# Keys of the pick stage read from PSUM instead of SBUF, with two product buffers instead of three

## The chip, the cores and the metric

The kernel runs on one core of one Trainium2 chip. The metric is device time in microseconds (us) of one execution, and smaller is better. The kernel before takes 2175.24 us, the median of 9 runs (2168.76 to 2190.18).

The engines are named as in the profile: PE (TensorE; PEld is its weight load), DVE (VectorE), ACT (ScalarE), POOL (GpSimd) and SP (SyncE, which here only issues DMAs).

## The reference

One graph layer over N = 6250 nodes and E = 200000 edges, sorted by their destination:

```python
w = silu(edge_attr @ W1 + b1) @ W2 + b2                 # (E, 9), edge_attr (E, 32)
h_src = features[src]                                    # (E, 64), rows of x
msg = einsum('ef,em,fmg->eg', h_src, edge_sh * w, W_tp)  # (E, 64)
agg = segment_sum(msg, dst, N) / sqrt(AVG_DEG)
emb = silu(c_noise[:, None] @ Wn1 + bn1) @ Wn2 + bn2     # gamma, beta per node
x = layernorm(x + agg * (1 + gamma) + beta)
```

The part that matters here is `features[src]`: for each edge a row of 64 floats is fetched by index.

## The kernel before, in words

The edges are cut into tiles of 128 and the tiles into 98 groups (`NBLK`) of 16 (`KB`). A group's source rows stand in one SBUF tile `hs` of 128 x 16 x 64 floats. They come there in three ways:

- by gather: `gather(g)` (line 101) issues one indirect DMA per tile on POOL, 1152 in all. Its tile `hs` has `AHEAD + 1` = 7 buffers, so the gathers of group i + 6 wait until PE has read group i - 1 (`windows`, line 611);
- by 128 single-row DMAs on SP for one tile of every fourth group (`load_rows`, line 117);
- by picking, for the last 4 tiles of a group (3 in group 0 and in the groups of `FEW`; 388 in all). All of x lies in SBUF, split into two parts `xs`. A source index is a pair: a key, which says in which of 7 x 128 rows a block of 7 nodes lies, and a number `jl` from 0 to 6 in the block.

A pick has three steps. `hots` (line 558, DVE) compares the 128 keys of a tile with `nk` for all 7 x 128 rows, which gives a 0/1 matrix `hot_k` of 128 x 896 (7 buffers). `pick` (line 573, PE) multiplies it with `xs` in 14 matmuls of 448 columns that add up in a PSUM tile `px`; `px` has 3 buffers, each one bank. Then DVE masks `px` with `jl` into `xm` (line 582) and sums `xm` over 7 into `hs` (line 584). When `xm` is written, the buffer of `px` is free.

The keys come from DRAM: `load_keys` (line 488) reads them as float16 for two groups at a time, the same on all partitions, into `kr` (2 buffers). Only groups 0 and 1 take theirs from PSUM (`keys_first`), where matmuls have written them as float32.

The remaining work of a group: `hidden` (line 505, PE, then Silu on ACT, lines 510 and 516), `second` (line 525), `weights` on DVE (its last step `a`, line 544), `windows` (line 611), which multiplies rows and weights into `pzw`, copies of `pzw` on ACT (line 625), `project` and `place` (lines 661, 665 and 675) for each pair of groups, and the ending of node blocks (lines 864 to 881).

The order of the work is written by hand (`tc.manual_schedule`); the engines work through it in that order, each on its own. One turn i of the main loop is, on PE: `pick(i+1, 0)`; `middle(i)`, which is `project` or its transpose, `hidden(i+2)`, `second(i+1)` and `windows(i)`; then `pick(i+1, 1)`, `pick(i+1, 2)` and `pick(i+1, 3)`. On DVE it is `hots(i+2)` for tiles 0 and 1, the mask and sum of pick 0, `hots(i+2)` for tiles 2 and 3, `weights(i+1)`, then the masks and sums of picks 1 to 3. On POOL it is the 11 to 13 gathers of group i + 6.

[...]

Of the kernel before, what the change touches and what calls it, by code (L numbers as in the profile page):

```python
# [7 lines left out]
F32 = mybir.dt.float32  # L8
# [8 lines left out]
P = 128  # L17
N, F, M, D, H, E = 6250, 64, 9, 32, 64, 200000
# [4 lines left out]
NBLK = (NT + KB - 1) // KB  # L23
W = 7
KW = KB * W
ZT = 8
# [3 lines left out]
Q = 4  # L30
J = 7
# [1 line left out]
SPG = range(7, NBLK, SPS)  # L33
SPR = P // SPS
EPS = 1e-5
FEW = range(NBLK - 7, NBLK - 2, 2)

KH = 8
NROW = NPAD + P
# [13 lines left out]
def picked(g):  # L53

    return Q - (g == 0 or g in FEW)

# [12 lines left out]
def gnn_resnorm_kernel(ctx: ExitStack, tc: tile.TileContext, x, src, dst, dst_row, ea, sh, cn,  # L69
                       w1, b1, w2, b2, wtp, wn1, bn1, wn2, bn2, out):  # L70
    nc = tc.nc
# [16 lines left out]
    with ExitStack() as fast:  # L88
# [4 lines left out]
        psum = fast.enter_context(tc.tile_pool(name="psum", bufs=1, space=bass.MemoryType.PSUM))  # L93
# [101 lines left out]
        def setup(temp):  # L195
# [68 lines left out]
            def keys_first(g, kf, pk, act=False):  # L264

                pk_t[g] = pk
                spread = []
                for t in range(picked(g)):
                    c = (g + 1) * Q - picked(g) + t
                    d0 = NBLK * KB + c * P  # L270
                    dg = xb.rearrange("p j f -> p (j f)")[:, d0:d0 + P]
                    if act:
                        nc.scalar.mul(dg, ident, kf[:, c:c + 1])
                    else:
                        nc.vector.tensor_scalar(dg, ident, kf[:, c:c + 1], None, op0=ALU.mult)
                    spread.append(lambda t=t, dg=dg: nc.tensor.matmul(pk_t[g][:, t, :], ones, dg,
                                                                      start=True, stop=True))
                return spread
# [9 lines left out]
            kb = [ztw[:, k * LB * Q:(k + 1) * LB * Q] for k in range(6)]  # L288
# [3 lines left out]
                f()  # L292
            high(0)
            low(0)
            spread = keys_first(1, kb[0], psum.tile([P, Q, P], F32, tag="px", name="pk1", bufs=3), act=True)
            hots(0, 0, 1)
            for h in range(1, J):
                high(h)
# [62 lines left out]
            windows(0)  # L361
            second(1)
            hots(1, 3, Q)
            for k in range(2):
                nc.scalar.copy(ht[k][H:H + 1], ones[H:H + 1, None, :].to_broadcast([1, 4, P]))
            pick(1, 2)
# [183 lines left out]

        pk_t = {}

        def hots(g, t0, t1):

            for t in range(t0, min(t1, picked(g))):
                hot_k[g, t] = late.tile([P, J, P], F32R, tag="hot_k", name=f"hot_k{g}_{t}", bufs=7)
                keys = pk_t[g] if g in pk_t else kr_t[g]
                nc.vector.tensor_tensor(hot_k[g, t], keys[:, t, None, :].to_broadcast([P, J, P]),  # L558
                                        nk.unsqueeze(2).to_broadcast([P, J, P]), op=ALU.is_equal)

        def pick(g, t, other=()):


            other = [f for fs in other for f in fs]
            q = picked(g) if g < NBLK else 0
            if t >= q:
                for f in other:
                    f()
                return
            px = psum.tile([P, F, J], F32, tag="px", name=f"px{g}_{t}", bufs=3)  # L570
            for h in range(J):
                for i in range(2):
                    nc.tensor.matmul(px.rearrange("p f l -> p (f l)"), hot_k[g, t][:, h, :],  # L573
                                     xs[i][:, h].rearrange("p f l -> p (f l)"),
                                     start=(h == 0 and i == 0), stop=(h == J - 1 and i == 1))
                    if i == 1 and other:
                        other.pop(0)()
            for f in other:
                f()
            xm = late.tile([P, F, J], F32, tag="xm", name=f"xm{g}_{t}")  # L580
            c = (g + 1) * Q - q + t
            nc.vector.scalar_tensor_tensor(xm, li[:, None, :].to_broadcast([P, F, J]), jl[:, c:c + 1], px,  # L582
                                           op0=ALU.is_equal, op1=ALU.mult)
            nc.vector.tensor_reduce(hs[g][:, tiles(g) - q + t, :], xm, AX.X, ALU.add)  # L584
# [7 lines left out]
        def windows(g, k0s=None, last=None):  # L592

            nk = tiles(g)
            end = g == NBLK - 1
            hsg, ag = hs[g], a[g]
            z = zs[g] if g in zs else sums(g)


            for k0 in range(0, nk, ZT) if k0s is None else k0s:  # L600
                n = min(ZT, nk - k0)
                k1 = 0
                if last is not None:
                    n, k1 = (n, n - 1) if last else (n - 1, 0)
                pz = [pzw[k0 // ZT][:, 0:ZT // 2 * M * W].rearrange("p (k m w) -> p k m w", m=M, w=W)] * 2
                if end and last is not False:
                    pe = psum.tile([P, ZT // 2, M, W], F32, tag="px", name=f"pz{g}_{k0 + k1}_", bufs=3)
                    pz = [pe if last else pz[0], pe]
                for k in range(k1, n):
                    v = k % 2  # L610
                    mm = nc.tensor.matmul(pz[v][v * F:(v + 1) * F, k // 2].rearrange("p m w -> p (m w)"),  # L611
                                          hsg[:, k0 + k, :], ag[:, k0 + k].rearrange("p m w -> p (m w)"),
                                          start=True, stop=True)
                    if k0 + k == 0:

                        for d in hs_dma.pop(g)[(g not in SPG):]:
                            tc.add_manual_dep(mm.ins, d.ins.name, mybir.DependencyInfo(
                                mybir.DependencyClass.Sync, mybir.DependencyReason.DATA), reason="rows of the group")
                for v in range(2):
                    for h in range(2):  # L620
                        k = k1 + (v - k1) % 2
                        if k >= n:
                            continue
                        copy = nc.vector.tensor_copy if last is False else nc.scalar.copy
                        copy(  # L625
                            z[h * F:(h + 1) * F, 0:5 - h, k0 + k:k0 + n:2, :].rearrange("p m k w -> p k m w"),
                            pz[v][v * F:(v + 1) * F, k // 2:(n + 1 - v) // 2, h:M:2, :])
# [120 lines left out]
        with tc.manual_schedule(), tc.tile_pool(name="temp", bufs=1) as temp:  # L748
# [6 lines left out]
            for i in range(1, NBLK):  # L755
                if i + AHEAD < NBLK:
                    gather(i + AHEAD)
                if i % LB == 0 and i + LB < NBLK:
                    near(i + LB)
                if i % LB == 1 and i + 1 + LB < NBLK:  # L760
                    load(i + 1 + LB)
                    load_keys(i + 1 + LB)
                if i % 4 == 3 and i + 1 < NJ:
                    gate_load(i + 1)
                for g in SPG:
                    if AHEAD - SPS < g - i <= AHEAD:
                        load_rows(g, (AHEAD - g + i) * SPR)
                while tables:
                    tables.pop()()
                while stores:  # L770
                    stores.pop(0)()
                more = []
                if i + 2 < NBLK:
                    more = [lambda: hots(i + 2, 0, 2)]
                pick(i + 1, 0, [nodes(i), more])
                if i + 2 < NBLK:
                    hots(i + 2, 2, Q)
                if 56 <= i <= 58:
                    reach(i - 56)
                if i == NBLK - 2:  # L780
                    break
                reads = middle(i)
                if i % 4 == 1 and i - 1 < NJ:
                    gate_hidden(i - 1)
                pick(i + 1, 1, [weights(i + 1)])
                for f in reads:
                    f()
                beside = more_of.pop(i, [])
                n = -(-len(beside) // (Q - 1))
                for t in range(2, Q + 1):  # L790
                    for f in beside[(t - 2) * n:(t - 1) * n]:
                        f()
                    if t < Q:
                        pick(i + 1, t)
                    if t == 2 and i == NBLK - 3:
                        late_turn(i + 1, NBLK // 2 - 4)
                    if t in (2, 3) and ends:
                        ends.pop(0)()
                if i in (3, 5):
                    tables.append(keys_turn(LB + KC * (i - 1) // 2, kb[0], kt))  # L800
# [4 lines left out]
            nc.scalar.activation(root, eps, AF.Sqrt)  # L805
            windows(g - 1)
            pick(g, 1, [weights(g)])
            py = psum.tile([P, 1, F], F32, tag="s", name="py_l")
            for f in bring(q - 2, q - 1, py):
                f()  # L810
            finish(q - 2, q - 1, py)
# [249 lines left out]
```

## Time and profile before

| what | value |
|---|---|
| median of 9 runs | 2175.24 us (2168.76 to 2190.18) |
| the profiled execution | 2161.79 us, its span 2160.0 us |
| busy: PE / DVE / ACT / POOL | 1756.0 / 1233.8 / 515.4 / 1142.5 us |
| gathers (line 101) | 1152, mean 991 ns |
| picks' matmuls (line 573) | 5432, 1186.3 us busy |
| `hot_k` from `kr` (line 558) | 381, mean 1084 ns |
| mean granted clock of TensorE | 0.864 |

Each row of a group of instructions gives line, engine, operation and tiles (out<-in), count, then busy time and mean duration, then the time for which the engine sat idle just before them and what ended that. In the timeline a row gives the start and the duration in us, then engine, line and operation. "remote" is a wait whose releaser the profile doesn't know; "issue" is time in which the engine waited for nothing that the profile shows. Ends of matmuls are modelled.

### The profile page before, as it was taken

How to read it: one execution, taken by the hardware profiler on the slowest of the kernel's cores; microseconds unless marked ns; L12 is line 12 of the kernel's file. 1: busy time of each engine (PE TensorE's matmuls, PEld its weight loads, DVE VectorE, ACT ScalarE, POOL GpSimd, SP SyncE). 2: the span in 40 equal slices, each digit the busy share in tenths (PEclk: the TensorE clock that was granted, in tenths of full speed). 3: DMA queues.
4: the chain of work that ended last, by engine and by line, in shares of the span. 5: the costliest groups of instructions: out<-in, count | busy, mean ns of one | idle time of the engine just before them, and what ended most of it. 6: DMA issues, size and time to landing. Idle time of an engine off the chain costs nothing.

```text
span 2160.0 us, 37200 instructions
## 1 busy us (share of the span) xinstructions
PE 1756.0 (81%) x12273; PEld 1412.1 (65%) x12273; DVE 1233.8 (57%) x2228; ACT 515.4 (24%) x1427; POOL 1142.5 (53%) x1161
## 2 busy tenths in 40 slices
PE   4067888888888878888888888888888887888898
PEld 3056766666676767676767666666666666666677
DVE  3055565656565646556565556565646564646587
ACT  2022121312222212223122212121222121212233
POOL 7745546455555556455555554545555555555510
PEclk7568989899988989898989898988888988888899
DMA  4121211111121112111111111111111111111110
GB/s 127 35 61 40 59 36 42 45 49 40 39 56 41 38 39 59 35 41 39 57 37 39 48 45 36 39 38 54 37 39 50 42 37 38 54 38 36 39 44 5
DMA packets 89776, 95.75 MB, mean 44 GB/s; under 512 B 36504, under 2 KB 51050, under 8 KB 89578
## 3 DMA queue, kind: packets, MB, share of 16 engines
q1 hardware_dynamic: 52138, 53.89, 8.0%
q0 software_dynamic: 36864, 37.82, 7.8%
q8 instruction: 99, 1.62, 0.3%
q10 hardware_dynamic: 576, 1.61, 0.2%
q14 instruction: 99, 0.81, 0.1%
HBM read 91.49 MB, written 1.73 MB: 43 GB/s over the span
## 4 chain that ended last, share of the span: by engine, by line
PE 72%; issue 17%; another core or an unknown queue 4%; DVE 4%; POOL 2%; DMA 0%; ACT 0%; DVEq 0%; ACTq 0%; POOLq 0%
PE px L573 48%; PE pzw L611 7%; PE p L525 5%; PE p L661 4%; PE p L505 4%; PE pzw L505 2%; POOL hs L101 2%; DVE xm L582 1%; DVE hot_k L558 1%; DVE hs L584 1%; PE p L713 0%; PE ps L675 0%; DVE a L544 0%; PE p L690 0%
## 5 line engine op out<-in xcount | busy, mean ns | idle before, releaser
L101 POOL DMA_INDIRECT hs<-in_x_dram,src_i x1152 | 1141.2, 991 | 926.4 <-PE pzw L611 595.3
L573 PE MATMUL px<-xs_w,hot_k 128*128 128x448 f32 x5432 | 1186.3, 376 | 31.2 <-issue 29.0
L573 PEld LDWEIGHTS px<-xs_w,hot_k 128*128 128x128 f32 x5432 | 1042.2, 195 | 124.2 <-issue 35.0
L582 DVE SCALAR_TENSOR_TENSOR xm<-li,jl,px 128x448 f32<-128x448 f32 x388 | 262.9, 678 | 849.0 <-remote 591.3
L558 DVE TENSOR_TENSOR hot_k<-kr,nk 128x896 fp32r<-128x896 f16 x381 | 397.5, 1084 | 0.0
L510 ACT ACTIVATE st<-p,b1c 128x512 f32<-128x512 f32 x98 | 67.4, 688 | 798.1 <-remote 439.4
L584 DVE TENSOR_REDUCE hs<-xm 128x64 f32<-128x448 f32 x388 | 240.6, 620 | 13.4
L625 ACT COPY ztw<-pzw 64x140 f32<-64x140 f32 (+1 forms) x778 | 209.3, 269 | 45.3 <-PE pzw L611 32.9
L661 PE MATMUL p<-ztw,wtc 128*64 128x112 f32 x940 | 107.8, 328 | 128.5 <-issue 128.2
L505 PE MATMUL pzw<-ea,w1bd 32*64 32x256 f32 x784 | 130.9, 541 | 96.5 <-issue 95.7
L611 PEld LDWEIGHTS pzw<-a,hs 128*64 128x64 f32 x3116 | 153.4, 198 | 84.0 <-issue 82.5
L611 PE MATMUL pzw<-a,hs 128*64 128x63 f32 x3116 | 170.5, 289 | 13.8 <-issue 11.3
L661 PEld LDWEIGHTS p<-ztw,wtc 128*64 128x64 f32 x940 | 76.9, 174 | 155.6 <-issue 152.4
L525 PE MATMUL p<-st,w2p 128*32 128x256 f32 x784 | 123.3, 569 | 52.0 <-issue 45.0
L505 PE MATMUL p<-ea,w1bd 32*64 32x256 f32 x784 | 118.8, 520 | 54.4 <-issue 54.2
L505 PEld LDWEIGHTS pzw<-ea,w1bd 32*64 32x64 f32 x784 | 39.0, 167 | 128.1 <-issue 128.1
L544 DVE TENSOR_TENSOR a<-oh,p 128x1008 f32<-128x1008 f32 x98 | 117.9, 1203 | 3.3
L525 PEld LDWEIGHTS p<-st,w2p 128*32 128x32 f32 x784 | 26.6, 132 | 139.6 <-issue 113.1
L681 ACT COPY carry<-ps 128x128 f32<-128x128 f32 x48 | 12.8, 266 | 433.7 <-remote 402.5
L505 PEld LDWEIGHTS p<-ea,w1bd 32*64 32x64 f32 x784 | 35.8, 162 | 81.8 <-issue 77.8
L516 ACT ACTIVATE st<-pzw,b1c 128x256 f32<-128x256 f32 x196 | 82.4, 471 | 5.0 <-remote 2.4
L528 ACT ACTIVATE p2s<-p,b2c 128x256 f32<-128x256 f32 x98 | 46.3, 472 | 47.1 <-remote 23.9
(176 smaller groups left out, 556.7 us busy)
## 6 DMA issues: line engine op xcount, KB each, us to landing
hs<-in_x_dram SPq DMA_DIRECT2D x2944, 0.2 KB
ea<-in_ea_dram SPq DMA_DIRECT2D x48, 512.0 KB
hs<-in_x_dram,src_i POOLq DMA_INDIRECT x1152
kr<-kd SPq DMA_DIRECT2D x48, 256.0 KB
sh<-in_sh_dram SPq DMA_DIRECT2D x49, 144.0 KB
cb<-cn_d SPq DMA_DIRECT2D x12, 128.0 KB
out_dram<-o SPq DMA_DIRECT2D x23, 64.0 KB
dst_i<-in_dst_dram SPq DMA_DIRECT2D x1, 768.0 KB
```

What stands on the lines that cost most here:

```text
L101: hs_dma[g] = [nc.gpsimd.indirect_dma_start(out=hs[g][:, t - g * KB, :], out_offset=None, in_=x, in_offset=bass.IndirectOffsetOnAxis(ap=sr ...
L505: nc.tensor.matmul(half[q][s * H:(s + 1) * H].rearrange("p (c t e) -> p c t e", c=4, t=2), w1bd[q * D:(q + 1) * D, (q % 2) * H:(q % 2 + 1) ...
L516: nc.scalar.activation(st[g][:, 2 + q], pzw[q][:, 2 * P:], AF.Silu, bias=b1c)
L525: nc.tensor.matmul(p2[g][c * D:(c + 1) * D, 0, :].rearrange("p (q e) -> p q e", q=4), w2p, s[:, :, c * 2 * D:(c + 1) * 2 * D], start=True, ...
L544: nc.vector.tensor_mul(a[g], oh_t.pop(g)[:, :, None, :].to_broadcast([P, KB, M, W]), sw.unsqueeze(3).to_broadcast([P, KB, M, W]))
L558: nc.vector.tensor_tensor(hot_k[g, t], keys[:, t, None, :].to_broadcast([P, J, P]), nk.unsqueeze(2).to_broadcast([P, J, P]), op=ALU.is_equal)
L573: nc.tensor.matmul(px.rearrange("p f l -> p (f l)"), hot_k[g, t][:, h, :], xs[i][:, h].rearrange("p f l -> p (f l)"), start=(h == 0 and i ...
L582: nc.vector.scalar_tensor_tensor(xm, li[:, None, :].to_broadcast([P, F, J]), jl[:, c:c + 1], px, op0=ALU.is_equal, op1=ALU.mult)
L584: nc.vector.tensor_reduce(hs[g][:, tiles(g) - q + t, :], xm, AX.X, ALU.add)
L611: mm = nc.tensor.matmul(pz[v][v * F:(v + 1) * F, k // 2].rearrange("p m w -> p (m w)"), hsg[:, k0 + k, :], ag[:, k0 + k].rearrange("p m w ...
L625: copy(z[h * F:(h + 1) * F, 0:5 - h, k0 + k:k0 + n:2, :].rearrange("p m k w -> p k m w"), pz[v][v * F:(v + 1) * F, k // 2:(n + 1 - v) // 2 ...
L661: nc.tensor.matmul(pt[h * F:(h + 1) * F], wtc2[:, c, :], z[h][:, c], start=(c == 0), stop=(c == 4))
```

## The change

`hots` now always reads its keys from a PSUM tile. For groups from 2 on, a new function `keys(g)` copies the float16 keys of a group from `kr` on ACT into a float32 tile `pk` of 128 x 4 x 128 (one bank), at the top of the turn in which the group's `hots` begin; in the first turns it stands in `setup`. The bank for it has the new tag `r`, and `px` gives up one: 2 buffers instead of 3. The two PSUM tiles that used the tag `px` for other things (`pk1` in the setup, `pz` at the end) follow: `pk1` goes to `r`, `pz` has 2 buffers. `py_l` at the end moves from `s` to `r`. `FEW` has one group more (89), so there are 387 picks, and one gather more.

```diff
-FEW = range(NBLK - 7, NBLK - 2, 2)
+FEW = range(NBLK - 9, NBLK - 2, 2)
...
-            spread = keys_first(1, kb[0], psum.tile([P, Q, P], F32, tag="px", name="pk1", bufs=3), act=True)
+            spread = keys_first(1, kb[0], psum.tile([P, Q, P], F32, tag="r", name="pk1"), act=True)
...
             hots(1, 3, Q)
+            keys(2)
...
+        def keys(g):
+
+            pk_t[g] = psum.tile([P, Q, P], F32, tag="r", name=f"pk{g}")
+            nc.scalar.copy(pk_t[g][:, 0:picked(g), :], kr_t.pop(g))
+
         def hots(g, t0, t1):
 
             for t in range(t0, min(t1, picked(g))):
                 hot_k[g, t] = late.tile([P, J, P], F32R, tag="hot_k", name=f"hot_k{g}_{t}", bufs=7)
-                keys = pk_t[g] if g in pk_t else kr_t[g]
-                nc.vector.tensor_tensor(hot_k[g, t], keys[:, t, None, :].to_broadcast([P, J, P]),
+                nc.vector.tensor_tensor(hot_k[g, t], pk_t[g][:, t, None, :].to_broadcast([P, J, P]),
                                         nk.unsqueeze(2).to_broadcast([P, J, P]), op=ALU.is_equal)
...
-            px = psum.tile([P, F, J], F32, tag="px", name=f"px{g}_{t}", bufs=3)
+            px = psum.tile([P, F, J], F32, tag="px", name=f"px{g}_{t}", bufs=2)
...
-                    pe = psum.tile([P, ZT // 2, M, W], F32, tag="px", name=f"pz{g}_{k0 + k1}_", bufs=3)
+                    pe = psum.tile([P, ZT // 2, M, W], F32, tag="px", name=f"pz{g}_{k0 + k1}_", bufs=2)
...
                 more = []
                 if i + 2 < NBLK:
+                    keys(i + 2)
                     more = [lambda: hots(i + 2, 0, 2)]
...
-            py = psum.tile([P, 1, F], F32, tag="s", name="py_l")
+            py = psum.tile([P, 1, F], F32, tag="r", name="py_l")
```

## The prediction

> **What bounds the kernel now.** I read the page first, for the engines and the chain, then the waits, then the timeline of single turns, and last the rows of `hot_k`.
>
> ```profile
> PE 1756.0 (81%) x12273; PEld 1412.1 (65%) x12273; DVE 1233.8 (57%) x2228; ACT 515.4 (24%) x1427; POOL 1142.5 (53%) x1161
> PE 72%; issue 17%; another core or an unknown queue 4%; DVE 4%; POOL 2%; DMA 0%; ACT 0%; DVEq 0%; ACTq 0%; POOLq 0%
> L101 POOL DMA_INDIRECT hs<-in_x_dram,src_i x1152 | 1141.2, 991 | 926.4 <-PE pzw L611 595.3
> L573 PE MATMUL px<-xs_w,hot_k 128*128 128x448 f32 x5432 | 1186.3, 376 | 31.2 <-issue 29.0
> ```
>
> The chain is PE's, but 17% of it is "issue": PE stands with nothing to wait for. POOL is idle for 595.3 us until PE's `windows` frees a buffer of `hs`. So neither engine is busy all the time, and the timeline must say who holds whom. One turn of it:
>
> ```profile
> 1002.90 11.47 PE L573 MATMUL px<-xs_w,hot_k 128*128 128x448 f32 x56
> 1003.26 0.95 POOL L101 DMA_INDIRECT hs<-in_x_dram,src_i  x1 [7.25 <-PE pzw L611]
> 1003.46 2.08 DVE L558 TENSOR_TENSOR hot_k<-kr,nk 128x896 fp32r<-128x896 f16 x2
> 1004.51 1.86 POOL L101 DMA_INDIRECT hs<-in_x_dram,src_i  x1 [0.30 <-issue]
> ...
> 1018.88 0.95 POOL L101 DMA_INDIRECT hs<-in_x_dram,src_i  x1 [0.31 <-issue]
> ...
> 1019.67 0.68 DVE L582 SCALAR_TENSOR_TENSOR xm<-li,jl,px 128x448 f32<-128x448 f32 x1 [4.42 <-remote]
> ...
> 1021.07 1.10 PEld L611 LDWEIGHTS pzw<-a,hs 128*64 128x64 f32 x26 [1.23 <-issue]
> ```
>
> `windows` ends and lets POOL's burst of 12 gathers go (1003.26). PE runs four picks (56 matmuls, 11.47 us) and then crawls, one or two instructions per 0.7 us, until 1021.07. The last gather has ended at 1019.83. After the crawl PE does the rest of the turn in 1.6 us and the next burst starts at 1022.63. This is the same in all turns. I measured it over 78 of them, from all rows of PE and POOL (a crawl: gaps over 600 ns between starts on PE): it begins a mean of 12.4 us after the burst's start, and it ends 17.17 us after it for 12 gathers, 1.48 us earlier for 11, with a scatter of only 0.13 us. The crawl is tied to the burst. I know no mechanism for it; I use it as the rows have it. A turn is thus 17.2 us up to the end of the crawl and 2 to 6 us of PE's remaining work, 21.4 us in the mean.
>
> Results of PE are also told late during the crawl and before it: in the waits, the mask waits 591.3 us for "remote".
>
> ```profile
> POOL hs L101 <- PE pzw L611: 595.3, 90, 18.8
> DVE xm L582 <- remote: 591.3, 103, 49.5
> DVE xm L582 <- PE px L573: 106.9, 47, 24.9
> ```
>
> **The change, part by part.**
>
> **1. Keys from PSUM, on DVE.** The view of the tile `hot_k` has both kinds already, since groups 0 and 1 read PSUM:
>
> ```profile
> L558 DVE TENSOR_TENSOR hot_k<-kr,nk x381: 1078/1084/1135, 136.9 to 2125.5; 128x896 fp32r<-128x896 f16 x191
> L558 DVE TENSOR_TENSOR hot_k<-pk,nk x4: 1070/1080/1085, 30.1 to 131.8; 128x896 fp32r<-128x896 f32 x4
> ```
>
> The medians are 1084 and 1080 ns: 380 x 4 ns = 1.5 us of DVE, which is 57% busy and not on the chain. I take 0. [...]
>
> **2. The gathers that `hot_k` holds up.** Of 1152 gathers 1009 take 940 to 950 ns; the others are up to 1868. The time above 945 ns is 53 us in all, and 48.2 us of it lie in the 164 gathers that overlap a `hot_k`. A gather that starts in the first 0.1 us of a `hot_k` from `kr` takes 1588 ns on average; the row at 1004.51 above is one (1.86 us). Of the 8 that overlap one from PSUM, 6 take 947 or 948 ns; the two others (1443 and 1396 ns) overlap subtractions of line 286 too. One of the 6:
>
> ```profile
> 30.10 1.08 DVE L558 TENSOR_TENSOR hot_k<-pk,nk 128x896 fp32r<-128x896 f32 x1
> 30.63 0.95 POOL L101 DMA_INDIRECT hs<-in_x_dram,src_i  x1 [0.30 <-issue]
> ```
>
> So POOL gets about 48 us back, 0.5 us per burst. What is that worth? The naive bound is all of it, -48 us, if the crawl's end simply follows the last gather. The rows say otherwise. In the fit above, 1 us of delay in a burst's first four gathers moves the crawl's end by only 0.57 us, in the last four by 0.05; with 33.6 us of early delay that is -19 us. But the same early delay lets PE get further before the crawl: by 36 instructions per us, and the work left after the crawl is then 1.33 us shorter per us. The net is that a turn is 0.8 us (error 0.3) *shorter* per us of early delay. The comparison without a fit: turns repeat in fours (`project`, the single-row loads); the means of the four kinds are 21.46, 21.15, 20.53 and 22.63 us over all turns, and 21.53, 21.24, 21.25 and 22.88 us over those whose gathers were not held up (under 0.2 us early and late). The mean difference is +0.28 us, x 91 turns = +26 us. These were sorted by what happened, not by an experiment, so I shrink it: +20 us, with ends -48 and +26.
>
> **3. Two `px` instead of three.** A pick now needs the mask of the pick two before it to be done. PE's order is pick 1, 2, 3 and 0 of the next group, so pick 0 waits for the mask of pick 2. I compared, for each of the 368 picks between the first and last turns, the start of its matmuls with the end of the mask two before. Picks 1 and 2 have 2 us to spare at least. Pick 3 would have waited 6 us in sum, pick 0 57 us, with 7.8 us the longest. A turn where it bites:
>
> ```profile
> 405.29 11.48 PE L573 MATMUL px<-xs_w,hot_k 128*128 128x448 f32 x56
> 410.35 0.67 DVE L582 SCALAR_TENSOR_TENSOR xm<-li,jl,px 128x448 f32<-128x448 f32 x1
> 417.18 0.68 DVE L582 SCALAR_TENSOR_TENSOR xm<-li,jl,px 128x448 f32<-128x448 f32 x1 [5.50 <-PE px L573]
> 419.40 0.95 POOL L101 DMA_INDIRECT hs<-in_x_dram,src_i  x1 [0.30 <-issue]
> ```
>
> The matmuls of pick 2 ended at 411.2, but the mask (second row of DVE) started at 417.18; pick 0, which began at 413.8, would have stood until 417.9. No gather was held up in this burst, and that is the rule: in the 41 turns with under 0.25 us of early delay the wait would be 1.30 us on average, in the 45 others 0.00. With part 2 all turns are of the first kind: 91 x 1.30 = 118 us of waiting on PE. What covers it is the crawl: pick 0 (2.9 us) has until about 17.2 us after the burst's start, and from the release times only 3.1 us in all 86 turns reach beyond. That makes 7 us for 91 turns of the first kind if the crawl covers all, 118 us if nothing. Covered is nearer to what the rows show; I take 12 us, since the mask's own signal passes through the same stretch. What is late next is the mask of pick 0 and behind it `hots` for tiles 2 and 3; those already start after the crawl.
>
> **4. The copy of the keys on ACT**, 96 times 128x512. Nearest rows: the Silu of 128x512 at 688 ns above, the copy of 64x448 at 561 ns below: 54 to 66 us of ACT, which is busy 24%. It stands behind the copies of `rt` or `r` (1047.52 in one turn) and before `carry`, which starts at the crawl's end; that idle time covers it, 6 us or more. It waits for `kr`, which SP requests some 24 us ahead, and for `hots` of the group before, done by 2 to 4 us after the burst's start. Behind a square root, which waits up to 11.8 us for DVE's variance, it comes later, but before DVE has done the mask of pick 3. If that cover were gone, 66 us. SP's `kr` load now waits for ACT rather than DVE, and earlier; SP's other DMAs keep their order. I take 0.
>
> **5. One pick less.** Group 89 saves 14 matmuls (2.9 us) on PE and costs a gather (1.48 us at the crawl's end): -1 us. `pk1`, `py_l` and `pz` move in places where their banks are free (the last `xm` ends at 2150.94, `pz`'s second buffer is written at 2151.74): 0.
>
> The sum is 0 + 20 + 12 + 0 - 1 = +31 us on an execution of 2161.8 us. That one lies 13 us under the median and under the lowest of the runs shown; I put the sum on the median: 2175.2 + 31 = 2206 us.
>
> **The rivals.**
>
> *POOL's time is returned* (faster). The crawl ends with the burst, and without the hold-ups the burst ends earlier. For it: the scatter of 0.13 us. Against it: 0.57 and 0.05 instead of 1, and the longer rest. It decides when the rest after the crawl doesn't grow. -19 to -48, with +7 for `px` and -1: 2133 to 2162 us, centre 2158.
>
> *All hidden* (no change). The hold-ups are worth as much as they cost (0), `px` costs the 7 us of the covered case, the pick -1: 2181 us.
>
> *`px` becomes the bound* (slower by more). The wait for the mask isn't covered, because the late signals of PE come still later when pick 0 has not been issued. Half of the 118 us on top of +26: 2260 us; all of it, 2319.
>
> **How the numbers follow.** Forecast 0.48, its own range 2188 to 2230; POOL's time returned 0.23; all hidden 0.14; `px` the bound 0.15. The range reaches into both sides: 2150 leaves out the lower third of the faster case (0.07), 2260 half of the slowest (0.08). The bound of 0.5%, about what can be told from no change, is 11 us: faster 0.23, same 0.15, slower 0.62.
>
> **What would show it.** `hot_k<-pk` at 1080 ns for all rows; the mean of a gather falls from 991 to about 950 ns and no row near 1.8 us is left; ACT gets 96 copies of 0.6 us; PE has waits of `px` for `xm` before pick 0, in more than half of the turns; crawls end 17.2 us after the burst's start, and the rest after them is about 0.5 us longer. The forecast is wrong if turns with fast gathers are shorter than 21.4 us, or if pick 0 ends after the crawl in most turns.

## The result, and the profile after

The changed kernel takes 2222.20 us (median of 10 runs, 2209.68 to 2251.90) against 2175.24 us: a ratio of 1.020, 95% interval 1.0175 to 1.0225. The highest of the ten was in a slower state of the chip and is not in the ratio. By the medians the kernel is 47 us slower; 31 us were forecast, in a range from 2150 to 2260 us. The profiled execution has a span of 2222.7 us, 62.7 us more than the one of before, which lies 13 us under its median.

The direction and the order of size were right, but the loss shows at the smaller of the two terms of the sum, the wait for two `px`. From the page of the changed kernel:

```profile
L101 POOL DMA_INDIRECT hs<-in_x_dram,src_i x1153 | 1090.5, 946 | 1038.3 <-PE pzw L616 713.1
L578 PE MATMUL px<-xs_w,hot_k 128*128 128x448 f32 x5418 | 1286.7, 394 | 340.9 <-DVE xm L587 268.0
L563 DVE TENSOR_TENSOR hot_k<-pk,nk 128x896 fp32r<-128x896 f32 x384 | 399.6, 1081 | 0.6 <-ACT pk L557 0.6
L557 ACT CAST pk<-kr 128x512 f32<-128x512 f16 x96 | 56.8, 591 | 16.1 <-issue 8.4
```

Gathers are fast now, 946 ns in the mean instead of 991, and POOL has saved 51 us of busy time. It gains nothing by that: it waits 713.1 us for `windows` instead of 595.3. The comparison of keys takes 1081 ns, against 1084 ns from SBUF before. New is the second line: PE stands 268.0 us ahead of the picks' matmuls, waiting for a mask (`xm`). The waits of the same kernel:

```profile
DVE xm L587 <- remote: 748.8, 134, 49.6
POOL hs L101 <- PE pzw L616: 713.1, 91, 19.1
PE px L578 <- DVE xm L587: 268.0, 76, 9.0
```

PE waits for the mask 76 times, up to 9.0 us, and the mask waits for PE ("remote") 748.8 us instead of 591.3. One turn from the timeline shows the ring:

```profile
1021.90 9.10 PE L578 MATMUL px<-xs_w,hot_k 128*128 128x448 f32 x42
1022.28 0.94 POOL L101 DMA_INDIRECT hs<-in_x_dram,src_i  x1 [7.01 <-PE pzw L616]
...
1033.02 0.68 DVE L587 SCALAR_TENSOR_TENSOR xm<-li,jl,px 128x448 f32<-128x448 f32 x1 [3.67 <-remote]
...
1033.76 1.12 PE L578 MATMUL px<-xs_w,hot_k 128*128 128x448 f32 x2 [2.76 <-DVE xm L587]
...
1035.85 3.94 PE L578 MATMUL px<-xs_w,hot_k 128*128 128x448 f32 x10
...
1040.05 1.18 PE L666 MATMUL p<-ztw,wtc 128*64 128x112 f32 x20
```

The 42 matmuls of picks 1 to 3 are done at 1031.0, those of pick 2 some 3 us earlier. But DVE hears of pick 2 only at 1033.02, and pick 0, which needs its buffer, starts at 1033.76. It ends at 1039.8, 17.5 us after the burst's start. The crawl would have been over by then: it no longer covers the wait.

The wait of 2.76 us is only half of the delay. Pick 0 itself takes 6 us here, because TensorE's granted clock is half in that stretch. Below are the windows of the same turn for the matmuls of `px` on PE (window, its length, busy time and number of matmuls, granted clock, DMA share, GB/s), then that of a pick 0 of before:

```profile
1021.90:1031.00 9.10, 9.10 (x42) 0.95 0.44 127
1031.00:1033.70 2.70, 0.00 (x0) 0.88 0.11 25
1033.70:1039.80 6.10, 6.00 (x14) 0.50 0.08 16
```

```profile
1011.50:1014.40 2.90, 2.87 (x15) 1.00 0.10 23
```

With the 3.1 us that pick 0 takes in before, it would have ended 14.6 us after the burst's start.

I measured the same over 85 turns of each profile, from all starts of pick 0 and all masks:

| mean over 85 turns | before | after |
|---|---|---|
| turn, us | 21.43 | 22.12 |
| gathers' delay in a burst's first four, sum, us | 31.9 | 0.1 |
| mask of pick 2 after the end of its matmuls, us | 1.45 | 5.56 |
| end of pick 0 after the burst's start, us | 11.74 | 16.42 |
| turns in which pick 0 ends after 17.2 us | 0 | 41 |
| pick 0 from its first matmul to the end of its last, us | 3.13 | 4.39 |
| granted clock during pick 0 | 1.00 | 0.75 |
| granted clock over the turn | 0.88 | 0.88 |

The 44 turns of after in which pick 0 ends in time are 21.06 us long, shorter than before; the 41 others are 23.26 us. 41 x (23.26 - 21.43) = 75 us and 44 x (21.06 - 21.43) = -16 us: 59 us, nearly the whole difference of the spans. From the other side: pick 0 reaches beyond 17.2 us by 107 us in sum (17.2 us is the crawl's end in the mean over the turns). Behind it PE needs 3.4 us to the end of such a turn, where before it needed 4.2 us from the crawl's end (21.43 - 17.2): 41 x 0.8 = 33 us come back, and 107 - 33 = 74 us are left.

In all of the 41 late turns pick 0 ran mostly at half clock (0.56 in the mean) and took 5.37 us. An estimate from the starts of pick 0: had it taken 3.13 us as in before, it would have reached beyond 17.2 us in 18 turns, by 38 us in sum instead of 107. So more than half of the overrun is the slower pick and not the wait alone. The clock over the whole turn is the same in both kernels; what differs is that a stretch of low clock now falls on pick 0. In the turn above it follows PE's stand, from 1033.08 on; that the stand is its cause is the order of the rows, and no run separates the two.

### The profile page after: what moved, and what is told of

Read it like the earlier page. It is cut to its first block, busy times and chain, and to the rows that moved or that the text cites. A ratio compares the mean times of both kernels' runs of the same rounds, so it can differ in the third digit from the quotient of the medians.

```text
span 2222.7 us, 37174 instructions
## 1 busy us (share of the span) xinstructions
PE 1693.8 (76%) x12259; PEld 1387.4 (62%) x12259; DVE 1229.9 (55%) x2225; ACT 564.1 (25%) x1523; POOL 1091.8 (49%) x1162
## 5 line engine op out<-in xcount | busy, mean ns | idle before, releaser
L101 POOL DMA_INDIRECT hs<-in_x_dram,src_i x1153 | 1090.5, 946 | 1038.3 <-PE pzw L616 713.1
L578 PE MATMUL px<-xs_w,hot_k 128*128 128x448 f32 x5418 | 1286.7, 394 | 340.9 <-DVE xm L587 268.0
L578 PEld LDWEIGHTS px<-xs_w,hot_k 128*128 128x128 f32 x5418 | 1086.6, 206 | 476.4 <-DVE xm L587 297.2
L587 DVE SCALAR_TENSOR_TENSOR xm<-li,jl,px 128x448 f32<-128x448 f32 x387 | 262.0, 677 | 930.4 <-remote 748.8
L563 DVE TENSOR_TENSOR hot_k<-pk,nk 128x896 fp32r<-128x896 f32 x384 | 399.6, 1081 | 0.6 <-ACT pk L557 0.6
L616 PEld LDWEIGHTS pzw<-a,hs 128*64 128x64 f32 x3116 | 117.9, 159 | 53.8 <-issue 53.8
L506 PE MATMUL pzw<-ea,w1bd 32*64 32x256 f32 x784 | 91.8, 476 | 60.7 <-issue 60.0
L616 PE MATMUL pzw<-a,hs 128*64 128x63 f32 x3116 | 132.3, 248 | 2.5 <-DVE a L545 2.5
L666 PE MATMUL p<-ztw,wtc 128*64 128x112 f32 x940 | 72.4, 278 | 48.5 <-issue 48.5
L526 PE MATMUL p<-st,w2p 128*32 128x256 f32 x784 | 75.6, 464 | 3.4 <-DVE yt L689 3.3
L557 ACT CAST pk<-kr 128x512 f32<-128x512 f16 x96 | 56.8, 591 | 16.1 <-issue 8.4
```

The lines of the kernel that those rows point to most:

```text
L101: hs_dma[g] = [nc.gpsimd.indirect_dma_start(out=hs[g][:, t - g * KB, :], out_offset=None, in_=x, in_offset=bass.IndirectOffsetOnAxis(ap=sr ...
L506: nc.tensor.matmul(half[q][s * H:(s + 1) * H].rearrange("p (c t e) -> p c t e", c=4, t=2), w1bd[q * D:(q + 1) * D, (q % 2) * H:(q % 2 + 1) ...
L526: nc.tensor.matmul(p2[g][c * D:(c + 1) * D, 0, :].rearrange("p (q e) -> p q e", q=4), w2p, s[:, :, c * 2 * D:(c + 1) * 2 * D], start=True, ...
L563: nc.vector.tensor_tensor(hot_k[g, t], pk_t[g][:, t, None, :].to_broadcast([P, J, P]), nk.unsqueeze(2).to_broadcast([P, J, P]), op=ALU.is_ ...
L666: nc.tensor.matmul(pt[h * F:(h + 1) * F], wtc2[:, c, :], z[h][:, c], start=(c == 0), stop=(c == 4))
```

## The experiments

Each group of runs had its own chip, with runs of the kernel before on the same one. The chips were of two kinds. On one kind the kernel before takes 2150 to 2175 us, as in the result above, and PE crawls in every burst; on the other it takes 1590 us, and PE does not crawl (gaps of 0.6 to 0.9 us between starts on PE, from 150 to 1400 us of the profile: 82 in `before` on the first kind, 2 in `px2_only` on the second). What a run says depends on that, so each is told with its own time of before. Four of the five groups landed on chips without the crawl.

**1. The same change on a chip without the crawl** (`after_again`, no edit).

> The changed kernel itself, beside the kernel before, on the chip of the experiments. Where PE does not crawl in the bursts (the kernel before at about 1590 us, as in the four runs above), POOL's time is on the path and the lost hold-ups are gained: 1460 to 1470 us, as with the doubled copies (1464.5 us), a ratio of 0.92. Where PE crawls (the kernel before at about 2175 us): 2210 to 2235 us, a ratio of 1.015 to 1.025.

Measured: 1463.82 us against 1590.25 us, a ratio of 0.920 (0.9185 to 0.9218). So the same two programs differ by +2% on one chip and by -8% on another. What bounds them there, the other runs tell; what makes the chips differ, none does.

**2. The two buffers of `px` alone** (`px2_only`, from before).

```diff
-            px = psum.tile([P, F, J], F32, tag="px", name=f"px{g}_{t}", bufs=3)
+            px = psum.tile([P, F, J], F32, tag="px", name=f"px{g}_{t}", bufs=2)
```

(`pk1` and `pz` likewise.)

> The kernel before with two buffers of px and nothing else changed: hots still reads kr, no copies on ACT, 388 picks. Theory A (the waits of px for the mask are the loss, because PE's signal of pick 2 comes late in a burst whether gathers are held up or not): nearly the whole loss is here, 2205 to 2222 us. Theory B (two causes together: the mask is told late only in bursts whose first gathers are not held up; some 45 of 86 bursts of before were such): about half of the loss, 2190 to 2205 us, and waits of px for xm of 100 to 150 us instead of the 268 us of the changed kernel. Theory C (px costs what the forecast gave it when hidden, 7 us; the loss is the lost hold-ups or the copies): 2175 to 2187 us.

Measured, on a chip without the crawl: 1592.10 against 1590.04 us, 1.0006 (0.9993 to 1.0019), nothing. All three theories had been written for a crawling chip, so the run decides none of them; it shows that two `px` cost nothing where masks come in time (on this chip 0.3 us after the modelled end of their matmuls in the mean). Its page also shows what bounds the kernel on such a chip (first the gathers and the picks' matmuls, then the chain by engine and by line):

```profile
L101 POOL DMA_INDIRECT hs<-in_x_dram,src_i x1152 | 1219.8, 1059 | 352.9 <-issue 317.5
L573 PE MATMUL px<-xs_w,hot_k 128*128 128x448 f32 x5432 | 1162.4, 372 | 5.6 <-DVE xm L582 4.2
PE 39%; POOL 36%; issue 13%; DMA 9%; DVE 2%; SPq 1%; POOLq 0%; ACT 0%; DVEq 0%
POOL hs L101 36%; PE px L573 30%; DMA hs<-in_x_dram,src_i 8%; PE pzw L611 3%; PE p L661 2%; PE p L505 1%; PE p L525 1%; SPq L117 1%; DVE hot_k L558 1%; PE ps L675 0%; DVE xm L582 0%; PE p L713 0%; DVE xs_w L286 0%; DVE a L544 0%; PE p L690 0%
```

POOL has no wait for `windows` here; all its idle time but 35 us is the 0.3 us between two gathers. The gathers are 36% of the chain and take 1059 ns in the mean, since they run all the time and so meet `hot_k` more often (270 of them, 157 on the crawling chip): 132 us above 945 ns instead of 53 us. The changed kernel on such a chip, the page of `after_again`:

```profile
L101 POOL DMA_INDIRECT hs<-in_x_dram,src_i x1153 | 1095.7, 950 | 353.3 <-issue 323.5
PE 84%; POOL 7%; DVE 3%; issue 3%; DMA 2%; ACT 0%; POOLq 0%; DVEq 0%; ACTq 0%
```

POOL's busy time falls by 124 us and the time by 126 us. There the hold-ups were on the path, and their full length is returned; then PE is the bound. (`px2_only`, 1592 us, stands here for before, 1590 us.)

The keys change not only their place but also their type, from float16 to float32. No run separates the two, but rows do in part: the subtractions of line 286, float32 with both inputs in SBUF, also hold gathers up, in the changed kernel too (a gather that overlaps only them takes 1657 ns in before and 1662 ns after).

**3. The copies** (`after_copy2`).

```diff
-            nc.scalar.copy(pk_t[g][:, 0:picked(g), :], kr_t.pop(g))
+            for k in range(2):
+                nc.scalar.copy(pk_t[g][:, 0:picked(g), :], kr_t[g])
+            kr_t.pop(g)
```

> The changed kernel with every copy of the keys made twice, 96 copies of 0.59 us more on ACT. The prediction's step 4 and theories A and B: within 5 us of the changed kernel, 2217 to 2227 us. If the copies are a cause (they stand before carry and before the Silu of hidden), 57 us more of ACT costs as much again as the first did: 2235 us or more.

Measured without the crawl: 1464.54 us (0.921, 0.9195 to 0.9225). On a second chip of that kind the changed kernel itself took 1463.82 us (experiment 1), so 56 us more of copies on ACT cost nothing there. On a crawling chip this wasn't run.

**4. A delay on POOL in early gathers** (`before_delay`, and `after_delay` with the same edit of the changed kernel).

```diff
+                if g > AHEAD and len(hs_dma[g]) == 2:
+                    nc.gpsimd.memset(idle, 0)
```

with `idle` a tile of 1 x 1000 bytes.

> The kernel before with one memset on POOL (1 partition, 1000 bytes) behind the second gather of every burst from group 7 on, so 91 early delays of a size that the trace will tell (0.5 to 1.5 us). If early delay of a burst shortens the turn (the fit of the prediction, 0.8 us per us): 30 to 70 us faster, 2105 to 2145 us. If the crawl's end follows the burst with 0.57 us per us and nothing is given back: 25 to 75 us slower, 2200 to 2250 us. If both cancel: 2165 to 2185 us.

> The changed kernel with the same memset on POOL behind the second gather of every burst. If an early delay lets PE tell the end of pick 2 in time (theory B), the wait of px for xm falls from 268 us to under 150 us and the time falls by 20 to 50 us, to 2172 to 2202 us. If signals are late in any case (theory A), the wait stays above 200 us and the time rises or stays, 2220 to 2280 us.

The memset takes 922 ns, 91 times 84 us. Without the crawl it makes before 44 us slower (1634.34 us, 1.0274, 1.0257 to 1.0291) and the changed kernel 71 us slower than experiment 1 has it (1534.87 us, 0.9649 of before, 0.9633 to 0.9665). That is POOL's time on the path, as in experiment 2: POOL has 45% of the chain in the first and 28% in the second. The question behind it, whether a plain delay does on a crawling chip what the hold-ups do, was put twice more:

> The changed kernel with the memset on POOL behind the second gather of every burst, once more, for a chip on which PE crawls (the kernel before at about 2150 to 2175 us). If delay of the burst's early gathers as such lets PE tell the end of pick 2 in time, the lag of its mask falls from 5.6 us in the mean to under 3 us, the wait of px for xm from 268 us to under 120 us, and the time to 2110 to 2170 us, at or below before. If it is not the delay but something else of hots from kr, the lag stays over 4.5 us and the time is 2200 to 2270 us. On a chip without the crawl: 1535 us as in the first run.

> The changed kernel with the memset on POOL behind the second gather of every burst, a third time, for a chip on which PE crawls (the kernel before at about 2150 to 2175 us). A plain delay does what the hold-ups did: the lag of the mask of pick 2 under 3 us in the mean, the waits of px for xm under 120 us, 2110 to 2170 us. It is something else of hots from kr: lag over 4.5 us and 2200 to 2270 us. On a chip without the crawl: 1535 us as in the two runs before.

Both landed on chips without the crawl: 1538.04 us (0.9655, 0.9639 to 0.9671) and 1534.31 us (0.9647, 0.9626 to 0.9667), as the first time. The question stays open.

**5. Half of the gathers** (`before_gather6`).

```diff
-                for t in range(g * KB + (g in SPG), g * KB + tiles(g) - picked(g))]
+                for t in range(g * KB + (g in SPG) + (6 if g > AHEAD else 0), g * KB + tiles(g) - picked(g))]
+            if g > AHEAD:
+                k = int(g in SPG)
+                nc.sync.dma_start(hs[g][:, k:k + 6, :], x[0:6 * P, :].rearrange("(p k) f -> p k f", k=6))
```

> The kernel before with 6 gathers of each group from 7 on replaced by one plain DMA of 6 tiles from SP (the rows are then not those asked for: the gather of these tiles is left out). If the crawl is tied to the burst of gathers, it ends 1.48 us earlier for each of the 6, at about 8.3 us after the burst's start, before the four picks are done, and so it disappears: 1450 to 1650 us where before takes 2175. If the crawl has another cause, it stays: over 2000 us. Where PE does not crawl at all (before at 1590 us), POOL leaves the path and PE is what remains: 1430 to 1500 us.

Measured without the crawl: 1455.65 us (0.9152, 0.9131 to 0.9173; two runs), in the range for such a chip. With POOL out of the way PE alone needs that (99% busy); the changed kernel is within 8 us of it. That the crawl is tied to the gathers could not be tried on a crawling chip.

**6. The reading of the keys alone, on a crawling chip** (`copy_unread`). The changed kernel, copies and two `px` included, but `hots` takes its keys from SBUF as before. The copies are read by nobody.

```diff
-            nc.scalar.copy(pk_t[g][:, 0:picked(g), :], kr_t.pop(g))
+            nc.scalar.copy(pk_t[g][:, 0:picked(g), :], kr_t[g])
...
-                nc.vector.tensor_tensor(hot_k[g, t], pk_t[g][:, t, None, :].to_broadcast([P, J, P]),
+                keys = kr_t[g] if g in kr_t else pk_t[g]
+                nc.vector.tensor_tensor(hot_k[g, t], keys[:, t, None, :].to_broadcast([P, J, P]),
```

> The changed kernel, but hots reads the keys from kr again (SBUF); the copies to pk are still made and read by nobody; px has 2 buffers, 387 picks. On a chip where the kernel before takes about 1590 us: if the hold-ups of gathers are the whole gain there, it goes back to 1585 to 1600 us, with gathers of 1050 to 1065 ns in the mean; if the copies, the pick or px have a part, it stays between 1480 and 1570 us. Where before takes about 2175 us: if px is the loss, 2195 to 2225 us; if the lost hold-ups are, 2170 to 2185 us.

This group landed on a crawling chip: 2139.75 against 2154.30 us, a ratio of 0.9907 (0.9861 to 0.9953). Neither expectation for such a chip held: two buffers, copies and one pick less together are no loss at all, but a gain of 0.9%. Page and waits:

```profile
L101 POOL DMA_INDIRECT hs<-in_x_dram,src_i x1153 | 1146.5, 994 | 893.7 <-PE pzw L617 568.4
L579 PE MATMUL px<-xs_w,hot_k 128*128 128x448 f32 x5418 | 1201.7, 379 | 85.2 <-issue 52.9
```

```profile
DVE xm L588 <- remote: 582.3, 102, 45.1
POOL hs L101 <- PE pzw L617: 568.4, 91, 17.3
PE px L579 <- DVE xm L588: 29.0, 20, 7.0
```

The gathers are held up again (994 ns), and PE waits 29.0 us for masks instead of 268.0, with the same two buffers. By the measure of the table above, the mask of pick 2 comes 1.42 us late in the mean, and pick 0 ends past 17.2 us in 5 of 85 turns instead of 41. Within this one profile, the 41 turns with early hold-ups (0.25 us or more) have a lag of 0.43 us and none of them is late; the 44 others have 2.34 us, and all 5 late ones are among them. So the loss on a crawling chip comes with the reading from PSUM: 0.991 without it, 1.020 with it on the first chip and 1.014 with it on this one (`few24` below, which also has 18 picks less). The waits and the late turns point to `px` as its way. That isn't shown by a run: reading from PSUM with three `px` wasn't tried; the changed kernel gives the place of the third to `pk`.

**7. Fewer picks** (`few24` on the same crawling chip, `few14` on one without the crawl).

```diff
-FEW = range(NBLK - 9, NBLK - 2, 2)
+FEW = range(NBLK - 45, NBLK - 2, 2)
```

> The changed kernel with 18 more groups of three picks: 369 picks, 18 gathers more. Where before takes about 1590 us the changed kernel is PE's (98% busy, chain 91% PE) and POOL has 1092 us of gathers and 309 us of issue between them in 1462 us: PE loses 18 x 2.8 = 50 us, POOL gains 18 x 1.25 = 22 us and becomes as long as PE: 1425 to 1445 us. If the waits between the two eat it: 1455 to 1475 us. Where before takes about 2175 us: a pick less saves PE 2.9 us and a gather more puts the crawl's end off by 1.48 us: 2190 to 2225 us.

Measured: 2186.98 against 2154.30 us, 1.0136 (1.0051 to 1.0221), 3 us under the range given for such a chip. It is the changed kernel with 18 picks less. On the chip on which `copy_unread` gained, it loses: fast gathers (948 ns) and late masks go together here too.

```profile
PE px L578 <- DVE xm L587: 125.9, 44, 7.2
```

The lag is 4.18 us in the mean, and 25 of 85 turns are late; they take 22.41 us, the others 21.29 us. The granted clock during pick 0 is 0.59 in the late turns here too.

`few14` has `NBLK - 29` in the same line.

> The changed kernel with 10 more groups of three picks: 377 picks, 10 gathers more. On a chip where PE doesn't crawl, where the changed kernel takes 1464 us: PE loses 10 x 2.8 = 28 us and POOL, with 12.5 us more, does not yet reach PE's time: 1434 to 1448 us. If waits between PE and POOL eat it: 1455 to 1470 us. Where PE crawls: between the changed kernel and the one with 369 picks, a ratio of 1.01 to 1.02.

Measured: 1476.65 us, 0.928 of before (0.9260 to 0.9300), 13 us more than the changed kernel; the 1434 to 1448 us I expected were a miss. PE is busy for 1421.3 us instead of 1437.2, but the waits take more than that back, as the answer on waits shows:

```profile
PE pzw L616 <- DMA hs<-in_x_dram,src_i: 25.9, 12, 4.2
PE pzw L616 <- DMA hs<-in_x_dram: 7.2, 3, 2.4
```

In `after_again` the first of these was 6.9 us. So in single turns a gather more makes `windows` wait for POOL's last rows, though POOL as a whole is not busier than PE (1103.3 us against 1421.3).

**8. Pick 0 behind `hidden` and `second`** (`pick0_late`), to take its wait out of PE's way.

```diff
-                pick(i + 1, 0, [nodes(i), more])
-                if i + 2 < NBLK:
-                    hots(i + 2, 2, Q)
...
+                for f in nodes(i) + more:
+                    f()
+
+                def first():
+                    pick(i + 1, 0)
+                    if i + 2 < NBLK:
+                        hots(i + 2, 2, Q)
...
             second(i + 1)
+            first()
             windows(i)
```

> The changed kernel with pick 0 of the next group moved on PE behind hidden and second, directly ahead of windows; the order on DVE stays. Where PE crawls: if the wait of pick 0 for the mask of pick 2 is the loss, PE does hidden and second in its place, the wait on PE falls to under 100 us and the time to 2120 to 2180 us; if the matmuls of pick 0 now fall into the crawl and are what is left after it, 2200 to 2280 us. Where PE doesn't crawl: PE's work is the same, 1455 to 1485 us; if windows now waits for the mask of pick 3, which pick 0 used to cover, 1490 to 1560 us.

Measured without the crawl: 1506.58 us, 0.9462 of before (0.9446 to 0.9478), 43 us more than the changed kernel. That is in the second of the two ranges for such a chip, but not for its reason: `windows` has no wait for a mask; PE's longest wait is that of `second` for `yt` on DVE, which the changed kernel doesn't have. The chain names the cost, DVE with 20% where the changed kernel had 3% (the wait stands last):

```profile
PE 61%; DVE 20%; POOL 9%; issue 5%; DMA 3%; SPq 2%; ACT 0%; POOLq 0%; DVEq 0%; ACTq 0%
PE px L578 48%; POOL hs L101 9%; PE pzw L616 4%; DVE hot_k L563 4%; DVE xm L587 4%; DVE hs L589 3%; PE p L526 3%; DMA hs<-in_x_dram,src_i 2%; PE p L506 2%; DVE a L545 2%; PE p L666 1%; SPq L117 1%; DVE p L540 1%; DVE c L650 1%; DVE p L536 1%
PE p L526 <- DVE yt L689: 25.8, 24, 2.3
```

What it would do on a crawling chip is not known.

Besides the two kernels themselves, no version was run on both kinds of chip. Of those that fetch all their rows none was faster than the changed kernel without the crawl; with it `copy_unread` was the fastest, of three.

## Why the prediction was right, and where it was not

- *Step 1, keys on DVE at nothing:* right. 1081 ns for 384 instructions, as forecast.
- *Step 2, the hold-ups:* right that the gathers fall to about 950 ns (946), that POOL's time is not returned on this chip, and that early hold-ups shorten a turn there. The size, +20 us, and the way were wrong. The +26 us behind it were +0.28 us per turn, the mean over four kinds of turns; 0.18 of the 0.28 came from one kind, of which only 3 turns were without hold-ups. It said that turns without hold-ups are longer as such; but the 44 turns whose pick 0 was in time are 21.06 us, shorter than the 21.43 us of before. The length came in only where the mask of pick 2 was late. Before's turns, sorted by hold-ups, had perhaps shown this effect while three `px` still softened it.
- *Step 3, two `px`:* the mechanism was named right (pick 0 waits for the mask of pick 2, in turns without hold-ups), and `copy_unread` shows the condition: with hold-ups the wait is 29.0 us. The step that failed is the sum behind it. It took 1.30 us of wait per turn, 118 us, from the 41 turns of before without hold-ups, and covered all but 12 us of it by the crawl. Measured are 268.0 us, and 107 us beyond 17.2 us. Two things in it were mis-sized. The lag: in before, the mask was 2.68 us late in such turns; in the changed kernel, where all are of that kind, it is 5.56 us. Why it doubles isn't shown; two `px` alone don't do it, since it is 2.34 us in such turns of `copy_unread`. And pick 0 itself: the sum gave it 2.9 us, but it took 4.39 us in the mean and 5.37 us in the late turns, at a granted clock of 0.56. The sum had no term for the clock.
- *Steps 2 and 3 were added, though the waits say that each sets the size of the other.* `px` with hold-ups, with the copies and one pick less, is -0.9%; on top of it, the reading from PSUM, with which the hold-ups go, brings the kernel to +2.0%. 1.020 / 0.991 is 3.0%, with the two intervals 2.4 to 3.5%: some 64 us for a term put at 20 us, while the rest was put at 11 us and is a gain of 20 us. (The two ratios are from two chips.) That the right total came out of these parts is luck. What the reading from PSUM would cost with three `px` isn't known, so the 64 us can't be split between the two steps.
- *Step 4, the copies:* their 591 ns were as bounded. They are inside the 0.9% gain of `copy_unread`, and a second set of them cost nothing without the crawl.
- *Step 5, one pick less:* too small to be seen by itself.
- *The rivals:* what happened lies between the forecast and "`px` becomes the bound": its mechanism, with 41 of 85 turns late instead of all, at less than its 2260 us. "POOL's time is returned" is wrong on the chip of the profile and right on the chips without the crawl, where 124 us of POOL's time returned 126 us. The prediction had this condition in its own words (the crawl and no known mechanism), but not the thought that it might belong to the chip and not to the kernel.
- *What would show it:* copies, gathers and waits came as listed. The crawl was still 17.3 us long where one is to be seen after pick 0, but over half of the 85 turns have no gap over 600 ns left there: pick 0 ends too late in them.

## What to carry to other kernels

A buffer taken away and a delay taken away need not be two terms to be added: where the delay made the slack that the buffer gave, one sets the price of the other, so measure the wait that the smaller buffer would have had in just the stretches that will be left. A wait's price can be more than its length: look at the granted clock of the work that comes behind it (here pick 0 took 5.37 us at 0.56 in the late turns, and 3.13 us at 1.00 in before). A stall that no row of the profile explains may belong to the chip; a term that rests on it holds only where it exists; here the same change gained 8% on chips without the stall and lost 2% on one with it. To tell two parts of a change apart, keep everything and give back one operand: `copy_unread` told the reading from the copies, the buffer and the pick in one run.

## What the runs showed of the hardware

- The same two programs ran on two kinds of chip: before took 2154 to 2175 us with a granted clock of 0.85 to 0.86, and 1590 us with 0.97 to 0.98. On the slower kind PE issues one or two instructions per 0.7 us late in each burst of gathers; on the faster kind the same bursts leave it alone (82 gaps of 0.6 to 0.9 us in before, 2 in `px2_only`, over the same stretch). What makes the difference isn't known.
- On the crawling chip DVE starts on a result of PE long after the matmuls' modelled end: for pick 2 by 5.56 us in the mean in the changed kernel, though DVE stood idle. In turns where an early gather was held up this lag of pick 2 is 0.35 us (before) and 0.43 us (`copy_unread`). That a delay of POOL as such does this was argued, not shown.
- The comparisons of 128x896 with both inputs in SBUF (1084 ns) held up the gathers that overlap them, 127 us in sum without the crawl (`px2_only`, where a gather takes 1059 ns in the mean); with the keys in PSUM, as float32 (1080 ns), they held up the 482 that overlap them by 4 us in sum (`after_again`, 950 ns).
- A matmul of a pick takes 365 ns (before) and 367 ns (after) in the mean at the full granted clock, and 610 and 592 ns at half. On the crawling chip the granted clock during pick 0 is under 0.75 in 50 of 85 turns of the changed kernel, in 7 of `copy_unread` and in none of before.
